# A check read off moved edges, columns made sooner, and the order of two arms

## Chip, cores, metric

One Trainium2 chip, one core. The time is device microseconds of one launch, a median over runs; beside it stands one execution taken with the hardware profiler. PE is the matrix engine (PEld its weight loads), DVE the vector engine, ACT the scalar engine, POOL the GpSimd engine, SP the engine that issues most DMAs. A "q" behind a name (SPq, POOLq) is that engine's sequencer.

## What is computed

Two layers of a graph network over 6250 nodes of 128 features and 106,250 directed edges, sorted by `dst`, self loops among them. Cut to what matters:

```python
h = relu(layernorm(x))
# layer 0: attention (GATv2)
xl, xr = h @ Wl + bl, h @ Wr + br
m = leaky_relu(xl[src] + xr[dst] + edge_attr @ We, 0.2)
logits = m @ att
ex = exp(logits - segment_max(logits, dst)[dst])
out = segment_sum(xl[src] * (ex / segment_sum(ex, dst)[dst])[:, None], dst) + bias_out
x = x + batchnorm(gelu(h + out))
h = relu(layernorm(x))
# layer 1: messages with a layer norm for each edge
em = relu(layernorm(concat(h[src], h[dst]) @ msg_w + msg_b)) * edge_weights[:, None]
messages = segment_sum(em, dst) / counts
h_new = relu(layernorm(concat(h, messages) @ upd_w + upd_b))
x = x + gate * h_new + (1 - gate) * h          # gate = sigmoid(h @ gate_w + gate_b)
```

## The kernel before

The edges are cut into NS = 99 blocks of BE = 1078. In a block the self loops are taken out and the other edges are moved together, so that SE = 1024 remain, eight tiles of 128; nodes' own edges are done apart. An edge's two numbers are packed into one integer in `ed_r` (the source in the upper bits, the node's distance from the block's first node in the lower seven). The moving together is done in seven steps, `squeeze(a, k)`: a predicated DVE copy that moves by 2^k places what the mask `moves[:, k]` marks. The same masks later squeeze the edge attributes `ea_r` and `own_r`. A block's nodes are fetched as two runs of NW = 40 rows, one for each half of the moved edges (CH = 512 edges to a half).

**The stage ahead** (lines 212 to 454) runs 17 batches of three node tiles in rounds `i` = 0 to 18: `normal(i)` normalises (ACT, PE transposes), `product(i - 1)` multiplies by `w0c` on PE, `table(i - 2)` copies the result into `tl` (ACT; DVE for the last four batches) and writes it to the table `xl_d`. Between them run generators, one step a round: `squeezing` (DVE; builds `ed_r` and `moves`), `statistics` (DVE), `checks` (POOL and ACT; twelve columns `bad` that say whether the graph fits the quick path) and `verdict` (adds up `bad` into `flag`). `columns_of(q)` turns half of the packed edges so that an edge is a partition, and makes `src_c`, the indices for the gathers. The order within this stage is the text's (a region of manual schedule).

**Two arms.** Every engine loads `flag` (line 1798) and branches (line 1799): `fast()` for graphs that fit, as these inputs do, `general()` otherwise. In the instruction streams the first arm stands right behind the branch, and a second branch at its end leads over the other arm.

**fast().** First part (1030 to 1090): the nodes' numbers within a block go to DRAM as `dl_d`, the two runs' first nodes as `base_d` and back into a row on SP (`base_row`); four node tiles of `xr` are written to `xr_d` in three bf16 parts (`part_rows`); `ea_r` is squeezed and split into three bf16 parts `ea_p`, which three DMAs write to `ea_d`, eight rows for a block; then the loads of blocks 0 and 1 are issued. `load_nodes` fetches a block's rows `W` and its `oht`, `load_weights` the eight rows from `ea_d`, and `one_hot_t` (DVE, line 1026) makes the one-hot of `oht`.

First sweep (1151 to 1457), round `s`: SP issues the loads of block s + 2; POOL issues eight gathers of `xl_d` rows into `gl` (line 185; ten buffers); PE multiplies the next block's one-hots (`spread`, line 1124); DVE adds `gl` (L1412), does the one-hot of block s + 2, multiplies by `att8` (L1422), reduces (L1424) and adds (L1428). Seven rounds later the block's weighted sum follows (L1393, L1407, L1437). `paced` makes a gather of block s wait for a mark of block s - 3: the first for L1412, the third for L1422, the fifth for L1428, the seventh for L1393 of the round behind. Small work is handed out over the rounds by generators: `begun` (`breaks`: where nodes begin, through `fst_d`, `brk_d`, `kbrk`, `brks`), `late` (`late_columns`), `made` (further rows of `xr_d`), `group` (finished nodes); in rounds 0 to 4 SP also issues four zeroings (`zero`). The order on each queue is the text's within a manual region; before, there are three of these regions in `fast()`, with a few instructions between the second and the third (`cen`, `avg`, `wm`, lines 1462 to 1469).

After the sweep a stage on all nodes (1484 to 1575) makes the tables of layer 1, and a second sweep (1579 to 1794) runs over the edges with gathers from `a_d`.

Of the kernel before, what the change touches and what calls it, by code (L numbers as in the profile page):

```python
# [9 lines left out]
F32 = mybir.dt.float32  # L10
BF16 = mybir.dt.bfloat16
I32 = mybir.dt.int32
U8 = mybir.dt.uint8
AF = mybir.ActivationFunctionType
# [3 lines left out]
P = 128  # L18
# [48 lines left out]
def kernel(  # L67
# [36 lines left out]
    def flat(v, ap, offset=0):  # L104
        return bass.AP(tensor=v.tensor, offset=v.offset + offset, ap=ap)
# [100 lines left out]
    def squeeze(a, k):  # L206

        w = 1 << k
        lo = CUTS[k] - w + 1 if k in CUTS else w
        V.copy_predicated(a[:, lo - w : BE - w], moves[:, k, lo:], a[:, lo:BE])  # L210

    with tc.tile_pool(name="pre", bufs=3) as pp, tc.tile_pool(name="pre1", bufs=1) as p1, tc.tile_pool(
# [135 lines left out]
        def checks():  # L348
# [4 lines left out]

            acc = p1.tile([NS, 3], F32, name="acc")
            junk = p1.tile([NS, RE - 1], BF16, name="junk")
            GP.tensor_tensor(own, own, step[:, 1 : BE + 1], ALU.add)
            GP.tensor_tensor(own, own, step[:, :BE], ALU.mult)

            place = p1.tile([NS, BE], F32, name="place")
            behind = p1.tile([NS, BE], F32, name="behind")  # L360
            GP.iota(place, pattern=[[1, BE]], base=0, channel_multiplier=0, allow_small_or_imprecise_dtypes=True)
            GP.tensor_scalar(behind, dst_r[:, :BE], base_f, None, op0=ALU.subtract)
            GP.tensor_tensor(place, place, behind, ALU.subtract)
            GP.tensor_scalar(place, place, float(CH), None, op0=ALU.is_le)
            GP.tensor_tensor(place, place, step[:, :BE], ALU.mult)
            far = p1.tile([NS, 6], F32, name="far")
# [24 lines left out]
            yield  # L391
            S.activation(junk[:, :BE], place, AF.Copy, accum_out=acc[:, 2:3])
            GP.tensor_tensor(q, far[:, 0:1], acc[:, 2:3], ALU.subtract)
            GP.tensor_scalar(bad[:, 11:12], q, float(NW - 1), None, op0=ALU.is_gt)

# [4 lines left out]
            yield  # L400

        def verdict():
            flag_ps = ps_k.tile([1, 12], F32, name="flag_ps", tag="ctp")
            T.matmul(flag_ps, ones[:NS, 0:1], bad, start=True, stop=True)
            yield
            V.tensor_reduce(sum_, flag_ps, AX.X, ALU.add)
            V.tensor_scalar(sum_, sum_, 0.0, None, op0=ALU.is_equal)
            yield
            S.copy(flag, sum_)
# [23 lines left out]
        for i in range(n + 2):  # L433
            if i % 2 and (i + 1) // 2 in rstds:
                scales((i + 1) // 2)
            if i < n:
                normal(i)
            next(stats, None)
            next(work, None)
            if i % 3 == 2:  # L440
                next(work, None)
            if 1 <= i <= n:
                product(i - 1)
            if i == 14:
                for _ in work:
                    pass
            if i in (15, 16):
                columns_of(i - 15)
            if i in (1, 4, 9):
                next(seen)  # L450
            if i >= 11:
                next(said, None)
            if i >= 2:
                table(i - 2)
# [469 lines left out]
    def fast():  # L924
# [9 lines left out]
        res0_d = [dram.tile([NP + P, WF], F32, name=f"res0_{i}") for i in range(2)]  # L934
        ea_d = dram.tile([NS * 8 * SE], BF16, name="ea_d")
        base_d = dram.tile([NS * 2], I32, name="base_d")
        fst_d = dram.tile([NS * SE], BF16, name="fst_d")
# [43 lines left out]
        rstd_c = fs.tile([P, NT], F32, name="rstd_c")  # L981
        gate = fs.tile([P, NT], F32, name="gate")
        bns = fs.tile([P, NGR, 6], F32, name="bns")
        g0 = ExitStack()
# [35 lines left out]
        def load_weights(s):  # L1020

            nc.sync.dma_start(ohts[s % 3][KW:P, :], flat(ea_d, [[SE, 8], [1, SE]], s * 8 * SE))

# [4 lines left out]
        dl_i = ed_r[:, :SE]  # L1028
        wins = {}
        with tc.tile_pool(name="col1", bufs=1) as p1, tc.tile_pool(name="ps_p", bufs=2, space=PSUM) as ps_p, tc.tile_pool(  # L1030
            name="ps_x", bufs=1, space=PSUM
        ) as ps_x, tc.manual_schedule():
            ps = ps_x.tile([P, TN, D], F32, name="xr_ps")
# [17 lines left out]
            nc.sync.dma_start(base_row, flat(base_d, [[0, 1], [1, 2 * NS]]))  # L1051
            squeeze(ea_r, 0)
            made = xr_rows(p1, ps, 0)
            next(made)
            for k in range(1, 3):
                squeeze(ea_r, k)
                V.tensor_tensor(we_l, We_r if k == 1 else we_l, we_p[:, k - 1, :], ALU.subtract)
                S.copy(we_p[:, k, :], we_l)
                next(made, None)
# [7 lines left out]
            for s in range(2):  # L1067
                wins[s] = load_nodes(xr_d, s)
            for k in range(3, 7):
                squeeze(ea_r, k)  # L1070
# [12 lines left out]
            S.copy(ea_p[2], rest)  # L1083
            for k, (r0, n) in enumerate(((0, 3), (3, 3), (6, 2))):
                nc.sync.dma_start(flat(ea_d, [[8 * SE, NS], [SE, n], [1, SE]], r0 * SE),
                                  ea_p[k][:, None, :].to_broadcast([NS, n, SE]))
            for s in range(2):
                load_weights(s)
                one_hot_t(wins[s][1])
            columns(ps_p, eac_c, ea_r, "ctp")  # L1090

# [59 lines left out]
        with tc.tile_pool(name="e0", bufs=2) as ep, tc.tile_pool(  # L1151
            name="e0o", bufs=2
        ) as op_, tc.tile_pool(name="e0m", bufs=2) as mp, tc.tile_pool(name="e0n", bufs=1) as np_, tc.tile_pool(
            name="ps_m", bufs=2, space=PSUM
        ) as ps_m, tc.tile_pool(name="ps_1", bufs=1, space=PSUM) as ps_1, tc.manual_schedule():
            (iota_ps,) = constants(ps_1)
# [143 lines left out]
            def breaks():  # L1300
# [7 lines left out]
                cut = ep.tile([NS, SE], BF16, name="cut", tag="oh")  # L1308
                V.tensor_scalar(cut, fst, -BIG, None, op0=ALU.mult)
                nc.sync.dma_start(flat(fst_d, [[SE, NS], [1, SE]]), cut)  # L1310
                yield
                brk = ep.tile([NS, 3, ST], BF16, name="brk", tag="glw")
# [5 lines left out]
                V.tensor_scalar(brk, brk, -BIG, None, op0=ALU.mult)  # L1318
                nc.sync.dma_start(flat(brk_d, [[ST, NS], [NS * ST, 3], [1, ST]]), brk)
                V.memset(kbrk[:, :, 0:1], 0.0)  # L1320
                V.memset(kbrk[:, :, P : P + 1], 0.0)
                for b, m, n in ((0, NBT, NS // SB), (NS // SB, NS % SB * ST, 1)):
                    if m:
                        nc.sync.dma_start(kbrk[:m, b : b + n, 1:P],
                                          flat(fst_d, [[P, m], [P * NBT, n], [1, P - 1]], b * P * NBT + 1))
                for q in range(2):
                    tp = ps_1.tile([P, 4, NS], F32, name="ctp", tag="np")
                    for j in range(4):
                        T.transpose(tp[:, j, :], fst[:, (q * 4 + j) * P : (q * 4 + j + 1) * P], ident[:NS, :NS])
                    S.copy(fst_c[:, :, q * 4 : (q + 1) * 4].rearrange("p s j -> p j s"), tp)  # L1330
                yield
                nc.sync.dma_start(brks, flat(brk_d, [[0, 1], [NS * ST, 3], [1, NS * ST]]))
# [7 lines left out]
            def late_columns():  # L1340

                def column(o, a):
# [4 lines left out]
                    for q in range(2):  # L1347
# [3 lines left out]
                        S.copy(o[:, :, q * 4 : (q + 1) * 4].rearrange("p s j -> p j s"), tp)  # L1351
                    yield
                V.tensor_add(bias_c, bias_c, bl_c)
                V.tensor_add(wlr, w0[:, :D], w0[:, D:])
                yield from column(own_c[0], own_r)
                nc.sync.dma_start(own_r, flat(edge_weight, [[BE, NS], [1, RE]]))
# [6 lines left out]
                yield from centred()  # L1363
                V.tensor_add(wab, w1[:, :D], w1[:, D : 2 * D])
                yield

# [10 lines left out]
            for s in range(NS + LAG + 1):  # L1377
# [71 lines left out]
                if group is not None:  # L1449
                    next(group, None)  # L1450
                if s < 3:
                    next(begun)
                else:
                    next(late, None)
# [7 lines left out]
        bn = fs.tile([P, 4], F32, name="bn")  # L1462
        cen = fs.tile([P, P], F32, name="cen")
        V.tensor_scalar(cen, ident, -1.0 / D, None, op0=ALU.add)
        avg = fs.tile([P, 1], F32, name="avg")
        V.memset(avg, 1.0 / D)
        wm = fs.tile([P, D + 1], F32, name="wm")
        V.tensor_copy(wm[:, :D], w1[:, :D])
        V.tensor_copy(wm[:, D:], w1[:, 3 * D : NW1])

# [11 lines left out]

        fx.enter_context(tc.manual_schedule())
        with tc.tile_pool(name="md", bufs=3) as mp, tc.tile_pool(
# [312 lines left out]

    usual = nc.values_load(flag[0:1, 0:1], min_val=0, max_val=1)
    with tc.If(usual != 0) as arm:
        fast()  # L1800
    with arm.Else():
        general()

# [40 lines left out]
```

## Time and profile before

| what | value |
|---|---|
| median of 3 runs | 2247.99 us (2247.89 to 2249.55) |
| the profiled execution's own time | 2248.83 us |
| its span | 2247.0 us, mean granted PE clock 0.651 |
| busy: PE, DVE, ACT, POOL | 1160.8, 1697.3, 1283.9, 1575.9 us |
| gathers, first sweep | 789, from 69.3 to 1083.9 us |
| gathers, second sweep | 789, from 1193.5 to 2188.7 us |
| HBM | 106 GB/s over the span |

Busy time is the time in which an engine executed something; the rest of the span it waited. A row of the timeline has the start (us from the span's beginning), the duration, the engine, the line of the kernel, the operation, what is written and read, and in brackets how long the engine was idle before and who let it go.

### The profile page before, as it was taken

The numbers are of one execution on the slowest core, as the hardware profiler recorded it, in microseconds if no ns is written. First come the engines' busy times: TensorE is split into PE (matmuls) and PEld (weight loads), VectorE is DVE, ScalarE is ACT, GpSimd is POOL, SyncE is SP. The second block draws the span as 40 slices with busy tenths as digits, with TensorE's granted clock in tenths as the row PEclk, the third lists the DMA queues.
The fourth block names the chain that finished last, engine by engine and source line by source line (L and its number), as shares of the span: only waits on it lengthen the run. The fifth ranks groups of instructions, "written<-read, shape, count | busy, mean of one in ns | idle before, by whom it ended". The sixth has DMA issues, their size and how long they took to land. (4 is left out here: it accounts for less than half of the span.)

```text
span 2247.0 us, 28217 instructions
## 1 busy us (share of the span) xinstructions
PE 1160.8 (52%) x6261; PEld 1032.2 (46%) x6261; DVE 1697.3 (76%) x3898; ACT 1283.9 (57%) x4314; POOL 1575.9 (70%) x1637
## 2 busy tenths in 40 slices
PE   5215545645555654655673445454554554554454
PEld 4114545544444544544553445454544554544443
DVE  8558887887787787777864677787787787788785
ACT  6214434444443444433435677777787787787774
POOL 6667777777777777777226777777777777777770
PEclk9556666665666566555676666666666665766776
DMA  5463356434444434434223333443443343343341
GB/s 139 143 187 100 94 150 187 123 93 113 114 94 115 111 88 114 118 84 107 49 61 104 87 104 94 106 113 93 107 109 101 96 115 106 87 117 104 95 106 30
DMA packets 243495, 239.16 MB, mean 106 GB/s; under 512 B 90708, under 2 KB 186909, under 8 KB 243315
## 3 DMA queue, kind: packets, MB, share of 16 engines
q1 hardware_dynamic: 192531, 133.21, 21.0%
q0 software_dynamic: 50496, 103.92, 19.7%
q14 instruction: 128, 1.05, 0.2%
q8 instruction: 52, 0.85, 0.2%
q10 hardware_dynamic: 288, 0.13, 0.0%
HBM read 189.20 MB, written 47.90 MB: 106 GB/s over the span
## 5 line engine op out<-in xcount | busy, mean ns | idle before, releaser
L185 POOL DMA_INDIRECT gl<-xl_d,src_c x789 | 767.2, 972 | 267.3 <-issue 162.2
L185 POOL DMA_INDIRECT gl<-a_d,src_c x789 | 752.7, 954 | 248.7 <-issue 166.4
L1437 PE MATMUL agg_ps<-glw,oh 128*128 128x131 f32 x1578 | 342.8, 403 | 217.0 <-ACT agg L1297 154.1
L1437 PEld LDWEIGHTS agg_ps<-glw,oh 128*128 128x128 f32 x1578 | 318.7, 306 | 238.3 <-ACT agg L1297 219.4
L1774 PE MATMUL agg_ps<-glw,oh 128*128 128x130 f32 x1056 | 240.9, 417 | 331.5 <-ACT glw L1765 331.5
L1774 PEld LDWEIGHTS agg_ps<-glw,oh 128*128 128x128 f32 x1056 | 222.5, 314 | 345.5 <-ACT glw L1765 345.5
L1745 ACT ACTIVATE sq<-y 128x128 f32<-128x128 f32 x789 | 243.8, 309 | 107.9 <-DVE y L1737 86.1
L1407 ACT ACTIVATE glw<-gl,exm 128x128 f32<-128x128 f32 x763 | 233.1, 389 | 0.0
L1413 ACT ACTIVATE m_ps<-m_ps 128x1024 f32<-128x1024 f32 (+1 forms) x99 | 99.5, 1005 | 218.0 <-DVE m_ps L1412 109.9
L1412 DVE TENSOR_TENSOR m_ps<-m_ps,gl 128x1024 f32<-128x1024 f32 (+1 forms) x99 | 121.7, 1230 | 123.6 <-DMA gl<-xl_d,src_c 107.3
L1756 DVE SCALAR_TENSOR_TENSOR y<-y,rs,cst 128x128 f32<-128x128 f32 x789 | 211.7, 341 | 0.0
L1774 PE MATMUL agg_ps<-ea_r,oh 128*128 128x130 f32 x522 | 120.4, 421 | 171.3 <-ACT ea_r L1765 171.3
L1124 PEld LDWEIGHTS <-oht 128*128 128x128 bf16 (+1 forms) x1578 | 146.2, 126 | 124.7 <-issue 55.5
L1774 PEld LDWEIGHTS agg_ps<-ea_r,oh 128*128 128x128 f32 x522 | 111.0, 318 | 177.9 <-ACT ea_r L1765 177.9
L1026 DVE TENSOR_SCALAR oht<-oht,third 120x1024 bf16<-120x1024 bf16 x198 | 100.1, 506 | 103.7 <-DMA oht<-dl_d 103.5
L1765 ACT ACTIVATE glw<-y,ew_c 128x128 f32<-128x128 f32 x528 | 161.5, 388 | 0.0
L1422 DVE TENSOR_TENSOR m_ps<-m_ps,att 128x1024 f32<-128x1024 f32 (+1 forms) x99 | 120.9, 1221 | 36.9 <-ACT m_ps L1413 36.2
L1745 ACT ACTIVATION_READ_ACCUMULATOR sq<-y 128x1 f32 x789 | 146.9, 186 | 0.0
L1737 DVE TENSOR_TENSOR y<-y_ps,gl 128x1024 f32<-128x1024 f32 (+1 forms) x99 | 119.4, 1206 | 33.2 <-DMA gl<-a_d,src_c 17.3
L1124 PE MATMUL m_ps<-W,oht 128*128 128x128 bf16 x789 | 89.2, 282 | 101.4 <-DVE lr L1424 83.0
L1761 ACT ACTIVATE y<-y 128x1024 f32<-128x1024 f32 (+1 forms) x99 | 104.3, 1054 | 37.6 <-DVE y L1758 37.6
L1424 DVE TENSOR_REDUCE lr<-m_ps 128x8 f32<-128x1024 f32 (+1 forms) x99 | 120.9, 1221 | 3.4
(329 smaller groups left out, 2247.2 us busy)
## 6 DMA issues: line engine op xcount, KB each, us to landing
oht<-dl_d SPq DMA_DIRECT2D x198, 240.0 KB
gl<-xl_d,src_c POOLq DMA_INDIRECT x789
gl<-a_d,src_c POOLq DMA_INDIRECT x789
res<-zt SPq DMA_DIRECT2D x20, 327.5 KB
res<-zt SPq DMA_DIRECT2D x20, 325.0 KB
res<-agg SPq DMA_DIRECT2D x99, 64.5 KB
res<-agg SPq DMA_DIRECT2D x99, 64.0 KB
W<-xr_d SPq DMA_DIRECT2D x198, 30.0 KB
```

The lines of the kernel that those rows point to most:

```text
L185: return GP.indirect_dma_start(out=dest, out_offset=None, in_=table, in_offset=bass.IndirectOffsetOnAxis(ap=idx, axis=0))
L1124: T.matmul(ps[:, j, :], oht[:rows_, j * P : (j + 1) * P], w[:rows_, j // TN, :], start=True, stop=True)
L1407: S.activation(glw[:, j, :D], glu[:, j, :D], AF.Copy, scale=f)
L1412: passed[s] = [V.tensor_tensor(ps, ps, gl[:, :n, :D], ALU.add)]
L1422: passed[s].append(V.tensor_tensor(ps, ps, over_tiles(att8, n), ALU.mult))
L1424: V.tensor_reduce(lr, ps, AX.X, ALU.add)
L1437: T.matmul(aggs[u], oh[:, j, :], glw[:, j, :], start=(j == 0), stop=(j == m - 1))
L1737: added = V.tensor_tensor(y[:, :n, :], pss.pop(s)[:, :n, :], gl[:, :n, :], ALU.add)
L1745: S.activation(sq, y[:, j, :], AF.Square, accum_out=rs[:, j : j + 1])
L1756: marks.append(V.scalar_tensor_tensor(yu[:, j, :], yu[:, j, :], ru[:, j : j + 1], mg_ps, op0=ALU.mult, op1=ALU.mult))
L1765: S.activation(glw[:, j, :D], yu[:, j, :], AF.Copy, scale=ew_c[:, u, j : j + 1])
L1774: T.matmul(aggs[u], oh[:, j, :], glw[:, j, :], start=(j == 0), stop=(j == m - 1))
```

## The change

- `checks`: five POOL operations over 1078 elements (`place`, `behind`), the ACT sum of `place` and its two POOL operations are left out. In their stead three DVE operations on one column take the number of the second half's first node from the squeezed `ed_r` and compare the same distance with NW - 1. That is a fourth step, in round 12.
- `verdict` begins in round 13 (11 before) and leaves out its comparison with zero: `flag` is now the sum of `bad`.
- `columns_of` runs in rounds 13 and 14 (15 and 16 before). The first three squeezes of `ea_r` move from the first part of `fast()` into rounds 16 to 18, ahead of `table`; squeeze 3 takes the place of squeeze 0 behind `dl_b`.
- The eight rows of the first four blocks go to a tensor of their own, `ea_h`, in three small DMAs, ahead of the loads of blocks 0 and 1; the three DMAs for all blocks follow behind these loads.
- `breaks` has four steps instead of three: each DMA stands a step behind the DVE work that it needs, and the eight small DMAs of the last step are issued in round 3 instead of 2.
- `late_columns` adds `bias_c` and `wlr` after its first column, and takes over `cen`, `avg` and `wm`, whose tiles are made at the beginning of `fast()`.
- `fast()` is one manual region from its first part on.
- `general()` is the first arm, `fast()` the second.

```diff
@@ checks @@
-            place = p1.tile([NS, BE], F32, name="place")
-            behind = p1.tile([NS, BE], F32, name="behind")
-            GP.iota(place, pattern=[[1, BE]], base=0, channel_multiplier=0, allow_small_or_imprecise_dtypes=True)
-            GP.tensor_scalar(behind, dst_r[:, :BE], base_f, None, op0=ALU.subtract)
-            GP.tensor_tensor(place, place, behind, ALU.subtract)
-            GP.tensor_scalar(place, place, float(CH), None, op0=ALU.is_le)
-            GP.tensor_tensor(place, place, step[:, :BE], ALU.mult)
...
-            S.activation(junk[:, :BE], place, AF.Copy, accum_out=acc[:, 2:3])
-            GP.tensor_tensor(q, far[:, 0:1], acc[:, 2:3], ALU.subtract)
-            GP.tensor_scalar(bad[:, 11:12], q, float(NW - 1), None, op0=ALU.is_gt)
...
+            half_i = p1.tile([NS, 1], I32, name="half_i")
+            V.tensor_scalar(half_i, ed_r[:, CH : CH + 1], P - 1, None, op0=ALU.bitwise_and)
+            more = p1.tile([NS, 1], F32, name="more")
+            V.tensor_tensor(more, far[:, 0:1], half_i, ALU.subtract)
+            V.tensor_scalar(bad[:, 11:12], more, float(NW - 1), None, op0=ALU.is_gt)
+            yield
@@ rounds of the stage ahead @@
-            if i == 14:
+            if i == 12:
                 for _ in work:
                     pass
-            if i in (15, 16):
-                columns_of(i - 15)
-            if i in (1, 4, 9):
+            if i in (1, 4, 9, 12):
                 next(seen)
-            if i >= 11:
+            if i in (13, 14):
+                columns_of(i - 13)
+            if i >= 16:
+                squeeze(ea_r, i - 16)
+            if i >= 13:
                 next(said, None)
@@ fast, first part @@
-            nc.sync.dma_start(ohts[s % 3][KW:P, :], flat(ea_d, [[SE, 8], [1, SE]], s * 8 * SE))
+            nc.sync.dma_start(ohts[s % 3][KW:P, :],
+                              flat(ea_h if s < SB else ea_d, [[SE, 8], [1, SE]], s * 8 * SE))
...
-            squeeze(ea_r, 0)
+            squeeze(ea_r, 3)
...
+            def send(d, s0, n):
+                for k, (r0, m) in enumerate(((0, 3), (3, 3), (6, 2))):
+                    nc.sync.dma_start(flat(d, [[8 * SE, n], [SE, m], [1, SE]], r0 * SE),
+                                      ea_p[k][s0 : s0 + n, None, :].to_broadcast([n, m, SE]))
+
+            send(ea_h, 0, SB)
             for s in range(2):
                 load_weights(s)
                 one_hot_t(wins[s][1])
+            send(ea_d, 0, NS)
@@ breaks @@
+                yield
                 nc.sync.dma_start(flat(fst_d, [[SE, NS], [1, SE]]), cut)
-                yield
...
-                nc.sync.dma_start(flat(brk_d, [[ST, NS], [NS * ST, 3], [1, ST]]), brk)
...
+                yield
+                nc.sync.dma_start(flat(brk_d, [[ST, NS], [NS * ST, 3], [1, ST]]), brk)
+                for b, m, n in ((0, NBT, NS // SB), (NS // SB, NS % SB * ST, 1)):
+                    if m:
+                        nc.sync.dma_start(kbrk[:m, b : b + n, 1:P],
+                                          flat(fst_d, [[P, m], [P * NBT, n], [1, P - 1]], b * P * NBT + 1))
                 yield
                 nc.sync.dma_start(brks, flat(brk_d, [[0, 1], [NS * ST, 3], [1, NS * ST]]))
@@ rounds of the first sweep @@
-                if s < 3:
+                if s < 4:
                     next(begun)
-                else:
+                if s >= 3:
                     next(late, None)
@@ the two arms @@
-    usual = nc.values_load(flag[0:1, 0:1], min_val=0, max_val=1)
-    with tc.If(usual != 0) as arm:
+    special = nc.values_load(flag[0:1, 0:1], min_val=0, max_val=12 * P)
+    with tc.If(special != 0) as arm:
+        general()
+    with arm.Else():
         fast()
-    with arm.Else():
-        general()
```

## The prediction

> **What bounds the kernel now.** Read first: the costliest groups of the page. POOL issues 789 row gathers in each of two sweeps over the edges, at 944 ns plus a 0.30 us gap, 1.25 us each.
>
> ```profile
> L185 POOL DMA_INDIRECT gl<-xl_d,src_c x789: 940/944/4148, 69.3 to 1083.9; - x198
> L185 POOL DMA_INDIRECT gl<-a_d,src_c x789: 940/944/1427, 1193.5 to 2188.7; - x198
>   DVE m_ps L1422: 12.1, 13
> ```
>
> These come from the view of the gather's own line. 789 x 1.25 = 986 us; the first sweep took 1083.9 + 0.9 - 69.3 = 1015.5. In each 100 us from 200 to 1000 it shows 77 to 80 gathers, no wait over the gap. So the first sweep is POOL's, and what moves its end is when the gathers start and what they lose before some 160 us. Next, therefore, the timeline of that stretch:
>
> ```profile
> 22.64 2.82 POOL L363 TENSOR_TENSOR place<-place,behind 99x1078 f32<-99x1078 f32 x1
> 23.86 2.83 DVE L210 COPY_PREDICATED ed_r<-moves,ed_r 99x1077 int32<-99x1077 uint8 x1
> 29.19 1.34 DVE L210 COPY_PREDICATED ed_r<-moves,ed_r 99x1076 int32<-99x1076 uint8 x1
> 29.30 0.30 ACT L312 ACTIVATE rstd<-mv,eps 128x6 f32<-128x6 f32 x1 [3.73 <-DVE mv L310]
> ...
> 59.08 0.86 DVE L417 CAST ed_c<-ctp 128x396 int32<-128x396 f32 x1 [6.51 <-PE ctp L415]
> 65.80 0.69 DVE L1039 TENSOR_SCALAR ed_r<-ed_r 99x1024 int32<-99x1024 int32 x1 [0.58 <-issue]
> 68.41 0.23 DVE L1464 TENSOR_SCALAR cen<-ident 128x128 f32<-128x128 f32 x1 [1.90 <-DMA xl_d<-tl]
> 69.31 1.45 POOL L185 DMA_INDIRECT gl<-xl_d,src_c  x1 [18.95 <-DVE first_i L1045]
> 72.32 4.15 POOL L185 DMA_INDIRECT gl<-xl_d,src_c  x1 [0.30 <-issue]
> ...
> 138.13 0.43 SPq L1337 DMA_DIRECT2D b_d<-zt  x1
> 140.58 1.02 SPq L1016 DMA_DIRECT2D W<-xr_d  x2
> 141.64 0.40 SPq L1017 DMA_DIRECT2D oht<-dl_d  x1
> 145.16 0.48 DVE L1026 TENSOR_SCALAR oht<-oht,third 120x1024 bf16<-120x1024 bf16 x1 [14.07 <-DMA oht<-dl_d]
> 147.06 0.94 POOL L185 DMA_INDIRECT gl<-xl_d,src_c  x1 [8.46 <-DVE m_ps L1422]
> ```
>
> (Start, duration, engine, line; in brackets the idle time before and its releaser.) Three losses. The start at 69.31: the last `tl` copy ends at 65.22, its write to xl_d has landed when `cen` is let go at 68.41, and POOL follows 0.9 later (I take that landing as releaser, not `first_i`). Fifty gathers then end at 138.60, 69.3 us instead of 62.5: 6.8 lost, all beside DVE work (4.15 instead of 0.94 for the third). Then 8.46 - 0.30 = 8.2 us of nothing: the pace rule holds the third gather of block 6 until L1422 of block 3; that stands on DVE behind the one-hot of block 5, which waits for a load that SP issues after twelve zeroings and small DMAs. Last, the view of the branch's line and of the closing line:
>
> ```profile
> L1799 DVEq COMPARE_BRANCH  x2: 51/53/55, 65.7 to 2240.1; - x2
> L1799 SPq COMPARE_BRANCH  x2: 46/48/49, 65.6 to 2241.2; - x2
> L1839 SPq EVENT_SEMAPHORE  x14: 17/28/28, 2243.7 to 2247.0; - x14
> L1839 DVEq DRAIN  x2: 10/34/58, 2243.0 to 2246.5; - x2
> ```
>
> The first branch falls through into fast() (DVE goes on 0.1 us later); the second, over general(), costs DVE 2243.0 - 2240.1 = 2.9 us and SP 2.5 (ACT 2.9, POOL 3.2, PE 3.5 by the same rows).
>
> **The change, part by part.** I sum against the profiled execution, 2248.83 us (span 2247.0), which is 0.84 above the median 2247.99.
>
> *Check of the second half.* Five POOL operations of 1078 elements (18.46 to 32.60, 13.9 us) and the ACT accumulation at L392 (1.10 + 0.19 = 1.3) go; three 99x1 DVE operations of about 0.15 come, where DVE later idles 6.51. From 20 to 34 us DVE is busy 13.90 of 14.00 us and ACT waits for it (3.73 above). DVE operations beside the removed ones are long: 2.83 against 1.34 for the squeeze, 1.73, 1.45 and 1.95 against 0.70 for `moves`, 0.91 against 0.17 at L318: 5.1 us. Against that, `own_r` (2.23 on POOL) moves forward to some 31 us; where it ran it stretched a squeeze to 1.86 (0.45 for that size at 172.41), so I take back 1.6. DVE gains 3.5; from 34 to 60 us ACT is busy 24.78 of 26 and gains its own 1.3: 4.8. Bounds: 1.3 (DVE's stretching has another cause) to 6.4.
>
> *Columns two rounds sooner, three squeezes of `ea_r` into rounds 16 to 18.* Cast and shift (0.86 + 0.37 each) leave the last copies; squeezes of 1.35 stand ahead of the copies of batches 14, 15, 16. On before's clock the second `ctp` is ready near 57.35; DVE then has 1.24 + flag sum 0.15 + three copies of 0.55 + three squeezes 4.05 + 0.29 = 7.4, so 64.7 instead of 65.22: 0.5 gained (between 3.5, no squeeze in the way, and -1). Start of the gathers: 69.3 - 5.3 = 64.0.
>
> *General arm first.* The far jump leaves the end and stands ahead of fast(). At the end: the last output is issued by 2241.17 and its packets end in the microsecond after 2243, but SP closes only at 2246.1 (DRAIN) with 0.9 behind it; without the jump it can close at 2243.5: 2.6 gained (0 to 3). At the start the same 2.5 to 3.5 falls on each engine. POOL has the flag by some 54 and 58 after the jump, needed at 63: nothing. DVE resumes at 60.0 + 0.7 (flag load) + 2.9 = 63.5; without cover this would cost 2.9.
>
> The row has a taken jump at 2.5 to 3.5 us. The Trainium skill (Runtime: NRT & Kernel Launch, Instruction fetch mechanics) says why it speaks against this edit: code is fetched ahead only in sequence, and a taken branch outside the two pages held must wait for its page. By that rule alone every engine pays at the front, and were POOL's on the path the sum below would be 3.2 us smaller; the trace agrees on the size and puts POOL's wait under the landing of xl_d.
>
> *Weights of four blocks by themselves.* The first products waited for 1.6 MB: third write issued 87.19, weights loaded 93.77, products 96.05. On DVE, 1.90 wait for `cen`, its row (0.23) and `wm`, and three squeezes (1.37 each) go, so the last cast of `ea_p` ends near 80.5 (87.15). A write of four rows should land in 2.3 us, as small loads do (bounds 2.0 and the 4.2 of base_d): weights issued 83.0, products 85.4, L1412 of block 0 at 86.5 (97.16). The full write, three DMAs of 0.3 on SP, then delays the loads of block 2: one-hot at 91.5 (98.30).
>
> *Early DMAs spread out.* fst_d goes a round later, brk_d and kbrk too, brks, five columns and two tails to round 3; so SP is never parked behind DVE work of its own round. By DVE's rows (1.23 for L1412, L1422, L1424, 0.5 one-hot, 0.7 tab_x, 3.0 and 1.1 for the two parts of breaks) rounds 1, 2, 3 begin at 98.8, 105.6, 111.5; SP's load for block 5 stands behind xr_d (112.2), zeroings (2.5) and kbrk (1.3), lands at 122, and L1422 of block 3 ends at 123.7. POOL wants it at 64.0 + 62.5 + 4.5 = 131.0. The moved eight DMAs (5.0, plus 2.0 for the xr_d tail to land) hit one round later: block 6's one-hot 133.5, L1422 of block 4 135.2, wanted at 141. So no stall, with 6 us to spare: 8.2 gained (0 if the chain is 15 later). Of the 6.8 lost beside DVE I keep 4.5, as four of seven squeezes still run there: 2.3 gained (0 to 5).
>
> *Moved at no cost:* cen, avg, wm (0.23, 0.06, 0.34) go into rounds where DVE waits for gathers; uncovered 0.6. The one written order changes little: rows already follow the text but for `cen`, `wm`, `cst` and load_weights.
>
> Sum: 4.8 + 0.5 + 2.3 + 8.2 = 15.8 in the first sweep, 2.6 at the end, 18.4: 2248.8 - 18.4 = 2230.4, and 0.84 less against the median: **2230**. Each gather after 160 us keeps its 1.25, so the gain is carried; the stage between the sweeps hangs on the last gather at 1083.9.
>
> **Rivals.**
> *The stall only moves.* The eight DMAs park SP in round 3 as they did in round 2. For: 5.0 + 2.0 us are still in line. Against: 6 us of slack. It keeps up to 8.2: 2238.
> *Dropping POOL's work relieves nothing:* for it, one squeeze (29.19) was short with L365 at its back. 1.3 + 0.5 in place of 5.3, so 3.5 less: 2234.
> *The start is hidden anyway:* something late in the sweep sets its end; only 2.6 stays, 2245. Against: no wait there.
> *Slower: code arrives late all along fast().* If the jump leaves the fetching out of step, each fetch may show. The trace has 180 instruction packets for 28217 instructions, an estimated 16 for POOL's 2436 records. At 3.2 each on POOL that is 51 us, 2280; from the sixth on it eats the 18.4. For: after the jump at the end a fetch follows within 3 us (queues 8 and 14). Against: in the long run of fast() before, gathers show only 0.30 gaps.
> The Trainium skill (Runtime: NRT & Kernel Launch, Instruction fetch mechanics) lets the fetching run ahead in sequence again behind a branch, so by it the first page alone would be late.
>
> **How the numbers follow.** Forecast 0.58, moved stall 0.15, no relief 0.13, hidden 0.06, slower 0.08. The forecast's own range is 2225 to 2236; with the moved stall and the other bounds 2224 to 2241. What can be told from no change is about 0.2%, 4.5 us: faster 0.87, same 0.05 (part of the hidden start), slower 0.08.
>
> **What would show it.** L210 of `ed_r` at 1.3 throughout; last `tl` copy near 60, first gather near 64; DVE's first row of fast() 3.5 us after that copy; products near 85; no gather idle over 1 us before 200; last gather near 1068; under 3 us between the last output's issue and the span's end. It is wrong if a gather still idles over 4 us after 100, if the first starts after 67, or if gaps over 0.3 appear through the sweep.

## The result, and the profile after

| | before | after |
|---|---|---|
| median of 4 runs beside each other | 2247.94 us (2246.44 to 2249.55) | 2230.66 us (2225.88 to 2233.61) |
| ratio, 95% interval | | 0.9921 (0.9901 to 0.9941) |
| profiled execution, span | 2248.83, 2247.0 us | 2232.3, 2230.5 us |

The kernel is 0.8% faster, and the 16.5 us between the two spans lie where the starts of the gathers in both traces put them:

| mark | before | after | gained so far |
|---|---|---|---|
| first gather | 69.31 | 64.78 | 4.53 |
| gather 45 (counted from 0) | 132.67 | 124.86 | 7.81 |
| gather 50, the third of block 6 | 147.06 | 131.26 | 15.80 |
| last gather of the first sweep | 1083.89 | 1068.66 | 15.23 |
| first gather of the second sweep | 1193.53 | 1179.15 | 14.38 |
| last gather of the second sweep | 2188.73 | 2172.94 | 15.79 |
| issue of the last output | 2240.88 | 2226.33 | 14.55 |
| end of the span | 2247.0 | 2230.5 | 16.5 |

So the gain is made by 132 us, kept within 1.4 us through 2100 us, and 2.0 us are added behind the last output. The timeline of the kernel after (start, duration, engine, line; in brackets the idle time before and its releaser):

```profile
22.66 1.37 DVE L210 COPY_PREDICATED ed_r<-moves,ed_r 99x1077 int32<-99x1077 uint8 x1
25.95 0.30 ACT L312 ACTIVATE rstd<-mv,eps 128x6 f32<-128x6 f32 x1 [0.55 <-DVE mv L310]
32.45 3.49 DVE L210 COPY_PREDICATED ed_r<-moves,ed_r 99x1070 int32<-99x1070 uint8 x1
...
60.32 0.28 DVE L342 COPY tl<-mm 128x129 f32<-128x129 f32 x1
63.40 0.69 DVE L1042 TENSOR_SCALAR ed_r<-ed_r 99x1024 int32<-99x1024 int32 x1 [2.79 <-issue]
64.78 1.21 POOL L185 DMA_INDIRECT gl<-xl_d,src_c  x1 [27.47 <-DVE first_i L1048]
...
83.67 2.07 PE L1130 MATMUL m_ps<-W,oht 128*128 128x128 bf16 x16 [4.68 <-issue]
84.77 1.23 DVE L1424 TENSOR_TENSOR m_ps<-m_ps,gl 128x1024 f32<-128x1024 f32 x1 [3.90 <-PE m_ps L1130]
...
115.68 0.42 SPq L1007 DMA_DIRECT2D xr_d<-tab_p  x1
118.18 1.12 SPq L1333 DMA_DIRECT2D brk_d<-brk  x1
119.41 2.62 SPq L1336 DMA_DIRECT2D kbrk<-fst_d  x2
123.07 0.99 SPq L1017 DMA_DIRECT2D W<-xr_d  x2
128.41 0.49 DVE L1028 TENSOR_SCALAR oht<-oht,third 120x1024 bf16<-120x1024 bf16 x1 [12.26 <-DMA oht<-dl_d]
128.81 1.23 DVE L1434 TENSOR_TENSOR m_ps<-m_ps,att 128x1024 f32<-128x1024 f32 x1
131.26 0.94 POOL L185 DMA_INDIRECT gl<-xl_d,src_c  x1 [0.30 <-issue]
```

The first squeeze takes 1.37 us, where it took 2.83 beside `place`, and ACT waits 0.55 for `mv` instead of 3.73. Now `own_r` runs beside the squeeze at 32.45 and stretches that one. DVE enters fast() 2.79 us late, behind the jump. The first gather's wait is put down to `first_i`, but the trace's record of DMA completions has the last piece of `xl_d`, issued at 60.63, complete at 63.81, and POOL goes 0.97 later; in the kernel before the same piece was complete at 68.09 and POOL went at 69.31, 1.22 later. The third gather of block 6 stands behind nothing but its gap. What POOL waited for between 80 and 200 us, before and then after (sum, times, longest):

```profile
POOL gl L185 <- issue: 21.0, 69, 0.3
POOL gl L185 <- DVE m_ps L1422: 8.8, 2, 8.5
```

```profile
POOL gl L185 <- issue: 22.9, 75, 0.3
POOL gl L185 <- DVE m_ps L1434: 0.6, 2, 0.3
```

L1434 is L1422 of before, and its wait of 8.5 us is gone. Last, the branch's line and the closing line of the kernel after (durations in ns, first and last start):

```profile
L1803 PEldq COMPARE_BRANCH  x1: 4161/4161/4161, 58.5 to 58.5; - x1
L1803 DVEq COMPARE_BRANCH  x1: 72/72/72, 59.5 to 59.5; - x1
...
L1843 SPq EVENT_SEMAPHORE  x14: 17/28/28, 2226.7 to 2230.4; - x14
L1843 SPq DRAIN  x3: 7/7/13, 2229.6 to 2229.9; - x3
```

There is one branch instead of two, at the front. PE stays in it for 4.2 us; the end follows the last output's issue by 4.2 us instead of 6.1.

### The profile page after: what moved, and what is told of

Read it like the earlier page. It is cut to its first block, busy times and chain, and to the rows that moved or that the text cites. A ratio compares the mean times of both kernels' runs of the same rounds, so it can differ in the third digit from the quotient of the medians.

```text
span 2230.5 us, 28198 instructions
## 1 busy us (share of the span) xinstructions
PE 1159.4 (52%) x6261; PEld 1028.7 (46%) x6261; DVE 1691.6 (76%) x3900; ACT 1282.8 (58%) x4312; POOL 1560.1 (70%) x1630
## 5 line engine op out<-in xcount | busy, mean ns | idle before, releaser
L1434 DVE TENSOR_TENSOR m_ps<-m_ps,att 128x1024 f32<-128x1024 f32 (+1 forms) x99 | 120.9, 1221 | 41.7 <-ACT m_ps L1425 41.0
L1741 DVE TENSOR_TENSOR y<-y_ps,gl 128x1024 f32<-128x1024 f32 (+1 forms) x99 | 119.4, 1206 | 35.0 <-PE agg_ps L1778 18.8
## 6 DMA issues: line engine op xcount, KB each, us to landing
res<-agg SPq DMA_DIRECT2D x99, 64.5 KB
```

The costliest lines, as they stand in the source:

```text
L1434: passed[s].append(V.tensor_tensor(ps, ps, over_tiles(att8, n), ALU.mult))
L1741: added = V.tensor_tensor(y[:, :n, :], pss.pop(s)[:, :n, :], gl[:, :n, :], ALU.add)
```

## The experiments

The runs lie on four chips, each with the kernel before beside them. It took 2845.7 us on that of e1 to e4, 2801.7 on that of e5, e8, e9 and base_after, 2846.2 on that of p1 and p2, and 2245.1 on that of p3 and p4. On the first three a time stands only against the runs of its own chip; base_after, the kernel after unchanged, has GpSimd waiting for VectorE through both sweeps. From these traces I use mainly the marks up to 95 us, where base_after's gathers and VectorE rows agree with the profile of after to within 0.6 us, and the end. Where e1, e3, e4 or p2 are set beside base_after, two chips are compared, and no kernel before was profiled on the three.

**The start: p1 and e5.** p1 takes the third check alone out of the kernel before:

```diff
-            GP.iota(place, pattern=[[1, BE]], base=0, channel_multiplier=0, allow_small_or_imprecise_dtypes=True)
...
-            GP.tensor_tensor(place, place, step[:, :BE], ALU.mult)
...
-            S.activation(junk[:, :BE], place, AF.Copy, accum_out=acc[:, 2:3])
-            GP.tensor_tensor(q, far[:, 0:1], acc[:, 2:3], ALU.subtract)
-            GP.tensor_scalar(bad[:, 11:12], q, float(NW - 1), None, op0=ALU.is_gt)
+            GP.memset(bad[:, 11:12], 0.0)
```

> The kernel before, with the third check alone taken away (the five GpSimd operations on place and behind, the ScalarE sum, the two small GpSimd operations; its entry of bad is set to 0, so nodes of a second half that span too far are not noticed). Columns, arms, stores of the weights and the order of the breaks stay as in the kernel before. Theory: the removed work bought nearly all of the earlier start (putting the five operations back into the kernel after cost 4.9 us): first gather 4.5 to 5 us earlier than the 69.3 of before. The order of SP's loads stays, so the wait of GpSimd at block 6 stays, 8 to 9 us where the kernel before has 8.5, and the time falls by 4.5 to 6 us. Rival: the wait at block 6 falls away with the earlier start too, and the time falls by 13 us or more.

First gather 64.71, 4.6 us earlier than in the kernel before. Ratio 0.9985 (0.9963 to 1.0007), within its uncertainty no change. POOL's waits for VectorE from 85 to 200 us stay, 17.4 + 6.2 us. The start belongs to this one edit, ScalarE's sum included; the stall does not go with it.

e5 puts the five POOL operations back into the kernel after:

```diff
             GP.tensor_tensor(own, own, step[:, :BE], ALU.mult)
+            place = p1.tile([NS, BE], F32, name="place")
+            behind = p1.tile([NS, BE], F32, name="behind")
+            GP.iota(place, pattern=[[1, BE]], base=0, channel_multiplier=0, allow_small_or_imprecise_dtypes=True)
+            GP.tensor_scalar(behind, dst_r[:, :BE], base_f, None, op0=ALU.subtract)
+            GP.tensor_tensor(place, place, behind, ALU.subtract)
+            GP.tensor_scalar(place, place, float(CH), None, op0=ALU.is_le)
+            GP.tensor_tensor(place, place, step[:, :BE], ALU.mult)
```

> The kernel after, with the five removed GpSimd operations on the 99x1070 tiles (place and behind: an iota, two subtractions, a comparison, a product) put back where they were; their result is not used, and the ScalarE sum over it stays away. Theory: what the removal bought at the start is mostly VectorE's time beside those operations. The squeezes and the cuts of the moves that run beside them take their old durations again (squeeze 0 of ea_r lies later now, so the moves 1.4 to 2.0 us for 0.7 and the comparison before them 0.9 for 0.2), less what own_r's product, pushed behind them, no longer costs: first gather 3.5 us later than in the kernel after (68.3 where that has 64.8). Rival, that removing the GpSimd work relieves nothing and that the rest of the change (columns, ScalarE's sum) moved the start: first gather within 0.7 us of the kernel after. The time follows the first gather, up to 3.5 us over the kernel after.

First gather 69.12, against 64.25 in base_after: 4.87 later, where I expected 3.5. The median is 5.7 us higher (2787.43 to 2781.74), but the ratios, 0.995 (0.9927 to 0.9972) and 0.9932 (0.9908 to 0.9956), are not told apart. VectorE's rows in its timeline:

```profile
21.60 1.73 DVE L282 TENSOR_SCALAR moves<-ed_r 99x1078 uint8<-99x1078 uint8 x1
24.04 2.84 DVE L210 COPY_PREDICATED ed_r<-moves,ed_r 99x1077 int32<-99x1077 uint8 x1
26.92 1.45 DVE L282 TENSOR_SCALAR moves<-ed_r 99x1078 uint8<-99x1078 uint8 x1
```

In base_after these take 0.71, 1.36 and 0.72. ScalarE's sum stayed away, and yet most of the difference is back: the last `tl` copy ends 4.0 us later (64.51 for 60.52), and the other 0.9 of the gather's 4.87 lie behind it, where this time the store took 3.35 us to complete instead of 2.75 and POOL followed 0.3 later. What ScalarE's own 1.3 us bought, this run does not separate.

**The order of the arms: e1 and e2.** e1 is the kernel after with the fast arm first, e2 the kernel before with the general arm first and without the comparison. The edit of e1, and of e2 the other way round:

```diff
-    special = nc.values_load(flag[0:1, 0:1], min_val=0, max_val=12 * P)
-    with tc.If(special != 0) as arm:
-        general()
-    with arm.Else():
-        fast()
+    usual = nc.values_load(flag[0:1, 0:1], min_val=0, max_val=1)
+    with tc.If(usual != 0) as arm:
+        fast()
+    with arm.Else():
+        general()
...
             V.tensor_reduce(sum_, flag_ps, AX.X, ALU.add)
+            V.tensor_scalar(sum_, sum_, 0.0, None, op0=ALU.is_equal)
```

> The changed kernel with the two arms as before: fast() first, and the comparison of the flag with zero back. Theory (the far jump is hidden at the front, and saved at the end): the first gather stays at 64.8 and the gathers keep their times; DVE's first row of fast() comes 0.6 us after its last tl copy instead of 2.8, the first products near 80.5 instead of 83.7; from the last output's issue to the end of the span 6.1 us instead of 4.2. Time 2232.7, that is 2.0 more than the changed kernel. Rival (the jump at the front lies on the path): the gathers come 2 to 3 us earlier and the time is 2228 to 2230. Rival (the order of the arms does nothing): 2230.7 and 4.2 at the end.

> The kernel before with the two arms exchanged alone (general() first, the flag as the sum). Theory: the first gather stays at 69.3, but DVE's chain of fast() starts 2.5 to 3.5 us later, and here the gathers of block 6 hang on that chain: their idle time grows from 8.5 to some 11.5 us; 2.0 us come off the end. Time 2248 to 2250 against 2247.9. Rival (hidden at the front here too): idle time 8.5, time 2246.

e1: ratio 0.9903 (0.9872 to 0.9935); e2: 0.999 (0.9969 to 1.0011). The times do not tell the arms apart; the traces do, at the front for e1 and at the end for both. From e1's timeline:

```profile
60.42 0.27 DVE L342 COPY tl<-mm 128x129 f32<-128x129 f32 x1
60.62 0.68 DVE L1043 TENSOR_SCALAR ed_r<-ed_r 99x1024 int32<-99x1024 int32 x1
64.27 1.31 POOL L185 DMA_INDIRECT gl<-xl_d,src_c  x1 [27.02 <-DMA base_d<-first_i]
81.59 1.86 PE L1131 MATMUL m_ps<-W,oht 128*128 128x128 bf16 x16 [5.33 <-DMA oht<-ea_h]
```

Without the jump VectorE goes on at once, 2.8 us earlier than in the kernel after, and the first products come 2.1 earlier; but the last piece of `xl_d` is complete at 63.31, and the first gather goes at 64.27, as in base_after (64.25). At the end e1 needs 6.1 us from the last output's issue, e2 3.6. So the new order gains some 2 us at the end, and in the kernel after its price at the front is covered by that landing. In the kernel before this is not shown: e2's first gather comes at 71.47, not at 69.3. Its last `tl` copy ended 1.5 later than in the kernel before (66.68 for 65.22), behind six matrix products that took 1.63 us for 0.91, and the store behind it was complete at 70.25. POOL's waits for VectorE before 200 us are 18.3 + 8.3 us there; without a profile of the kernel before on that chip, whether they grew cannot be told.

**The weights of four blocks: e4.** The kernel after with the full `ea_d` written ahead of the loads, without `ea_h`:

```diff
-        ea_h = dram.tile([SB * 8 * SE], BF16, name="ea_h")
...
-                              flat(ea_h if s < SB else ea_d, [[SE, 8], [1, SE]], s * 8 * SE))
+                              flat(ea_d, [[SE, 8], [1, SE]], s * 8 * SE))
...
-            send(ea_h, 0, SB)
+            send(ea_d, 0, NS)
             for s in range(2):
                 load_weights(s)
                 one_hot_t(wins[s][1])
-            send(ea_d, 0, NS)
```

> The changed kernel without ea_h: the three writes for all blocks go first, and blocks 0 and 1 load from ea_d. Theory: the writes take 6.5 us to land, the first products come near 88.8 instead of 83.7, but block 2's loads then no longer stand behind these writes, so the one-hot of block 2 is only 2.5 later (97 instead of 94.6), and of that 1.2 us is slack: the gathers idle 1 to 2 us, time 2232. Rival (the small write alone removes the stall): idle over 5 us, time 2236 or more. Rival (it hides behind the gathers): 2230.7.

```profile
87.22 0.61 SPq L1022 DMA_DIRECT2D oht<-ea_d  x2
89.13 1.87 PE L1128 MATMUL m_ps<-W,oht 128*128 128x128 bf16 x16 [10.50 <-issue]
```

The weights are issued at 87.22 and the products come at 89.13, where base_after has 81.83 and 83.48: `ea_h` brings the first products 5.6 us earlier. No more than that is shown: I expected the one-hot of block 2 to come 2.5 later without it, and it comes at 93.58 (94.47 in base_after); gather 50 goes at 144.37 (146.23), with waits of up to 8.4 us before 200 us. Ratio 0.9915 (0.9886 to 0.9944), not told apart from the kernel after's 0.9921.

**The order of the breaks: e3.** The kernel after with the old `breaks` (each DMA in the step of its DVE work; the edit's further lines move `brk_d` and `kbrk` up in the same way) and its old rounds:

```diff
-                yield
                 nc.sync.dma_start(flat(fst_d, [[SE, NS], [1, SE]]), cut)
+                yield
...
-                if s < 4:
-                    next(begun)
-                if s >= 3:
-                    next(late, None)
+                if s < 3:
+                    next(begun)
+                else:
+                    next(late, None)
```

> The changed kernel with breaks() and its rounds as before (fst_d in round 0, brk_d and kbrk in round 1, the eight small DMAs in round 2). Theory: SP is parked behind DVE's work of its own round again, one-hot of block 4 waits some 5 us, one-hot of block 5 comes near 135 instead of 128.4, L1434 of block 3 ends near 137, and the gathers, which want it at 131.3, idle for 5 to 6 us. Time 2236. Rival (the earlier start and the early weights alone took the stall away): no gather idle over 1 us, 2230.7.

The one-hot of block 3 comes at 112.39 (102.52 in the kernel after, 105.47 in base_after), but those of blocks 4 and 5 at 125.56 and 145.09 (127.71 and 144.34 in base_after), and gather 50 at 146.98 with 146.23; ratio 0.9938 (0.9911 to 0.9964). The waits from 100 us on are larger than the edit in both, so its share in removing the stall is not settled by this run.

**The wait at block 6: p4 and p3.** p4 is the kernel before, p3 the kernel after, each with the zeroings in rounds 3 to 7:

```diff
-                if s < 5:
-                    zero(res0_d, WF, 2 * s)
-                    zero(res0_d, WF, 2 * s + 1)
+                if 3 <= s < 8:
+                    zero(res0_d, WF, 2 * (s - 3))
+                    zero(res0_d, WF, 2 * (s - 3) + 1)
```

> The kernel before with the same move of the zeroings and nothing else. Theory: the wait of 8.5 us at block 6 of the kernel before was the same queue. First gather unchanged (69.3); the wait at block 6 falls to 2 us or less where transfers are fast (2241 for 2248, ratio 0.997), and where they are slow the waits before 200 us fall by about 10 us (ratio 0.995 to 0.997). Rival: the wait stays, since the one-hot comes behind other work of VectorE and other loads: ratio 1.000 within 0.001.

2241.02 us for 2245.09, ratio 0.9984 (0.9974 to 0.9994). First gather 69.24. The load of block 5 and the gather that waited, from p4's timeline:

```profile
135.85 1.03 SPq L1016 DMA_DIRECT2D W<-xr_d  x2
142.34 0.94 POOL L185 DMA_INDIRECT gl<-xl_d,src_c  x1 [2.41 <-DVE m_ps L1422]
```

The load goes 4.7 us earlier than before's 140.58, the wait falls from 8.46 to 2.41, and the time by 4.1; I expected 2 us or less and a ratio of 0.997, so it gave somewhat less. From the load's issue to the one-hot it is 4.60 us here and 4.58 in the kernel before, so the load itself was not slowed by the zeroings. The stall was the load of block 5 standing late in SP's queue, and what was taken off that queue came off the time. The 2.1 us left stand behind `xr_d` (129.81) and the eight small DMAs, which this kernel has in round 2.

> The kernel after, with the zeroings of the first sweep's two tables (four transfers of 327.5 KB in each of rounds 0 to 4, 6.6 MB in all) put into rounds 3 to 7. Theory: what holds the one-hots of blocks 4 and 5, and by them GpSimd at blocks 5 to 7, is SP's queue, in which the zeroings of rounds 0 to 2 stand ahead of the loads for blocks 3 to 5. Where transfers are slower (base_after waited 17.7 us for VectorE at these blocks before 200 us), the one-hot of block 4 then comes 10 us earlier (127.7 there) and GpSimd's waits before 200 us fall below 8 us: 8 to 15 us under the kernel after, ratio to the kernel before 0.987 to 0.990. Where transfers are as fast as in the profiles of before and after, there is no wait left to remove, and the time is that of the kernel after within 2 us. Rival: the store of ea_d (1.6 MB) and round 1's and 2's part of xr_d hold the loads, and the waits stay within 3 us of base_after's, ratio 0.993.

2227.84 us for 2245.09, ratio 0.9919 (0.9904 to 0.9934), as the kernel after. The one-hot of block 5 comes at 125.84 instead of 128.41 and buys nothing, since no gather waited for it.

**An earlier start still: e8, p2, e9.** e8 takes the three squeezes out of the last rounds of the stage ahead; p2 does so with the arms and the comparison of e1; e9 is e8 with round 2's zeroings and breaks right behind its loads:

```diff
-            if i >= 16:
-                squeeze(ea_r, i - 16)
...
-            squeeze(ea_r, 3)
+            for k in range(4):
+                squeeze(ea_r, k)
```

```diff
                     wins[s + 2] = load(xr_d, s + 2, True)
+                if s == 2:
+                    zero(res0_d, WF, 2 * s)
+                    zero(res0_d, WF, 2 * s + 1)
+                    next(begun)
...
-                if s < 5:
+                if s < 5 and s != 2:
                     zero(res0_d, WF, 2 * s)
...
-                if s < 4:
+                if s < 4 and s != 2:
                     next(begun)
```

> The kernel after, with the three squeezes of ea_r (k = 0, 1, 2) taken out of the last passes of the prologue's loop and put before the fourth in fast(), behind the columns of first nodes. Theory: the first gather waits for VectorE alone, so it goes at 61.5 (three squeezes of 0.7 to 1.4 us less before it); but VectorE, and SP's loads that the one-hots wait for, come no earlier, so the second use of the gather buffers (gathers 50 and 58, which in the kernel after have about 1.2 us to spare) waits about 2 us, and the time is that of the kernel after within 1.5 us. Rival: the start alone sets the time: 3.3 us under the kernel after, with no wait of GpSimd at blocks 6 and 7.

The first gather did not come earlier but at 64.97 (base_after 64.25); median 3.5 us above base_after. The ratio is 0.9948 (0.9929 to 0.9968), not told apart from base_after's. My theory of this run fell, though not by this run alone: VectorE enters fast() at 63.10, as in base_after (63.19), so its chain was not moved. From e8's timeline:

```profile
63.10 0.69 DVE L1040 TENSOR_SCALAR ed_r<-ed_r 99x1024 int32<-99x1024 int32 x1 [5.16 <-issue]
64.97 2.31 POOL L185 DMA_INDIRECT gl<-xl_d,src_c  x1 [27.65 <-DVE dl_b L1050]
```

The last `tl` copy ends 2.7 us earlier and the last piece of `xl_d` is issued at 58.22, but it is complete only at 64.00, 5.8 us later (3.2 in the kernel after). VectorE's branch comes at 58.3, and its first row in fast() 4.7 us later.

> The kernel after, with the three squeezes of ea_r put behind the start as in e8_squeezes_after_start, and with the fast arm put first again (comparison with 0 back). In e8 the last store of xl_d was issued 2.4 us earlier and landed no earlier (5.8 us after its issue for 3.2), while the instruction packets of the jump to fast() went over the same DMA engines. Theory: these packets held the store up; without the jump it lands 3.2 to 3.5 us after its issue, and the first gather goes at 62 to 63 (e8: 65.0). Rival: the last six tiles of xl_d, 0.84 MB in some 5 us, are bound by the transfer itself, and the first gather stays at 64 to 65 with no instruction packet in sight. Either way the wait at blocks 6 and 7 stays and the end is 2 us longer than in the kernel after, so the time is within 2 us of the kernel after.

The theory of p2 fell as well. One instruction packet instead of ten lies between 55 and 66 us, VectorE enters fast() at 58.36, and yet the last piece, issued at 58.13, is complete at 65.75, and the first gather goes at 66.71. The code was not what held the store, and VectorE's chain, 4.8 us earlier than in base_after, was not what the gather waited for. Thirteen of the piece's 16 completions are in by 63.4, the last three at 64.7 to 65.8; why these lag is open. The rival, that the transfers bind, gave 64 to 65; it is neither shown nor out. Ratio 0.9935 (0.9912 to 0.9959).

> As the run before, and in round 2 of the first sweep the four zeroings and the stores and loads of the breaks (brk_d, kbrk) are issued right behind the loads for block 4, not behind round 2's part of xr_d, for which SP waits 9.4 us on ScalarE in the kernel after. Theory: SP then issues the loads for block 5 at about 117.5 (123.1 in the kernel after), its one-hot comes at about 123 (128.4), and the slack before gathers 50 and 58 grows to some 5 us; so the earlier start is kept: 2 to 3.3 us under the kernel after, and no wait of GpSimd before 200 us. Rival: something else (products, ScalarE, the buffers of the one-hots) holds block 5, and the wait at blocks 6 and 7 stays as in the run before.

Block 5's load went at 136.37 (139.74 in base_after), not at 117.5, and gather 50 at 143.20 (146.23). The first gather comes at 63.13, but here the rows of the stage ahead lie 1.0 us earlier from the beginning (L277, which packs the edges, at 14.15, 15.14 in base_after), and the store took 5.05 us to complete, as it lagged in e8. Ratio 0.994 (0.992 to 0.9959), the median 1.7 us above base_after: no gain is shown, and none of these versions beats the kernel after.

**The reference: base_after.** No edit.

> The kernel after, unchanged, as the reference for the runs beside it: first gather 64.8, gather 50 at 131.3, and the ratio to the kernel before 0.992.

Ratio 0.9932 (0.9908 to 0.9956), first gather 64.25, but gather 50 at 146.23: on this chip the stall is there with the kernel after too. Its row and one of the rows behind it:

```profile
POOL gl L185 <- DVE m_ps L1434: 17.7, 3, 9.1
```

```profile
124.47 0.86 ACT L1331 COPY fst_c<-ctp 128x396 f32<-128x396 f32 x1 [8.95 <-remote]
```

The first is from the waits up to 200 us, the second from the timeline: ScalarE idles 8.95 us with a releaser that the trace of this core does not show.

## Why the prediction was right

The forecast was 2230, the median 2230.66. That close a hit is partly luck. The sum took 18.4 us off the span, and the two traces differ by 16.5; the median is as near as it is because it lies 1.6 under the profiled execution, for the 0.84 I took. In the first sweep the gain at gather 50 is 15.80 for the 15.8 of the sum, because a start 0.8 short and 0.8 too many for the first fifty gathers cancel. By its own steps:

- *Start, 5.3:* 4.53 measured. The rows of the stage ahead begin 0.56 later in the trace of after (L277 at 15.23 for 14.67); counted from there the last copy gains 5.2 and the gather 5.1. The landing of `xl_d` was rightly taken as releaser: in e1 and p2 VectorE enters fast() 2.6 and 4.8 us earlier than in base_after, and the gather is not earlier. The split was not right. With the same count the whole check is worth 5.2 at the last copy (p1) and the POOL operations alone 4.3 (e5), where I gave them 3.5; the 0.9 between may be ScalarE's sum (I gave 1.3) or not. The stretched rows that I added up to 5.1 make 5.26.
- *`own_r`, 1.6 taken back:* it costs 2.1 where it now runs (3.49 against some 1.4 undisturbed); e5 has such a cost too, at another row (2.85 for 0.69), so it cancels there. In e8 the squeeze began a little earlier against `own_r` and took 1.39, `own_r` 3.41 instead of 2.23, and the VectorE row behind it 1.98 for 0.17. The Trainium skill (SBUF — State Buffer, Who interferes with whom) has a VectorE instruction with two SBUF inputs contend with a GpSimd instruction that reads SBUF; the squeeze, with `moves` and `ed_r`, agrees at 2.84 against 1.36. The comparisons that write `moves`, from `ed_r` alone, are stretched as well (1.73 for 0.71), and that sentence does not cover them.
- *First fifty gathers, 2.3:* 3.1. Counted as in the prediction, to the end of the fiftieth, they take 66.2 us, 3.7 over 62.5, where I left 4.5.
- *Stall at block 6, 8.2:* gone. But L1422 of block 3 was to end 7.3 us before the gather that wants it, and that of block 4 5.8 (the 6 to spare); L1434 ends at 130.04 and 140.59 with the gathers at 131.26 and 141.81: 1.2 each. Two terms were mis-sized: the rounds come 2.5 to 3.4 later than worked out (101.39, 108.08, 114.92 for 98.8, 105.6, 111.5), behind block 2's one-hot at 94.55 and not 91.5; and `brk_d` and `kbrk` hold SP 3.9 us for the 1.3 I took. From there to the one-hot of block 5 it is 6.4 us, near the 6 that I left. The stall only moving, the rival at 2238, was nearer than its 0.15 said.
- *Weights, products at 85.4:* 83.67, and e4 shows `ea_h` to be what brings them. But block 2's one-hot, which the full write was to delay to 91.5, comes at 94.55.
- *End, 2.6:* 2.0. I expected under 3 us behind the last output (my own sum left some 3.5), and it is 4.2: the output is complete 2.46 us after its issue, at 2228.79, as in the kernel before (2243.33, 2.45), but SP's DRAIN comes 0.8 after that, at 2229.6, for which I had left 0.2, and 0.9 follow.
- *Jump, 2.9 for VectorE, hidden:* 2.79, and hidden. The Trainium skill (Runtime: NRT & Kernel Launch, Instruction fetch mechanics) has a taken branch out of the window wait for its page; e1 without it goes on at once, and in base_after 2.5 (POOL) to 4.8 us (ScalarE) pass between an engine's branch and its next row.
- The slower rival, code late all along, is out: from 80 us on no gather of the first sweep waits longer than 0.3, and in the second only three do, 1.4 at most.
- *Dropping POOL's work relieves nothing* and *the start is hidden anyway* are out too: e5 puts the start back by 4.87, and 15.23 of the gain still stand at the last gather of the first sweep.
- Not foreseen: 1.25 us lost between gather 50 and the last output: 0.57 in the rest of the first sweep, 0.85 between the sweeps and 1.24 behind the last gather, less 1.41 gained in the second sweep.

By parts, then, the start is shown to be the POOL work (e5, and p1 with ScalarE's sum), the end the order of the arms (e1, e2), the earlier products `ea_h` (e4). That the stall is a load late in SP's queue is shown (p4); how its removal in the kernel after divides between `ea_h`, the breaks and the later small DMAs is only argued, and neither e3 nor e4 settles it.

## What to carry to other kernels

Price an operation off the critical path by what it does to the rows beside it: in e5 five GpSimd operations that nobody waits for, put beside VectorE's rows, set the first gather back by 4.9 us. Before pulling work forward, find in the record of completions what the first instruction really waits for; the releaser that the wait names can be a neighbour in time (`first_i`), and moving that buys nothing. A stall in an engine may be one load behind bulk transfers in a queue, and reordering pays only as far as somebody waits.

## What was not expected of the hardware

The same kernel took 2230.7 us in the runs of the result and 2781.7 on the chip of base_after, with rows of the same length (the squeeze at 22.6 us 1.37 and 1.36 us) but GpSimd waiting 270 us for `y` of L1741 in place of 6 and engines idle with a releaser marked remote; the cause stays open. And a store of the same 64.5 KB was complete 2.8 us after its issue (before), 3.2 (after), 5.8 (e8) or 7.6 (p2). In the last two the four last pieces are issued within 2.1 us instead of 4.5; whether that is the cause no run settles.
